# Attention heads on one core: 64-row value sums, a ring of scores, and a few tiles turned on TensorE

## The chip, the cores and the metric

The kernel runs on one core of a Trainium2 chip. The metric is device time in microseconds (us) of one execution; lower is better. The engines are TensorE (PE: matmuls, with its weight loads shown as PEld), VectorE (DVE), ScalarE (ACT), GpSimd (POOL) and SyncE (SP), which here issues most transfers (DMA).

## The reference, cut to what matters

The network has two layers over 3327 nodes with 256 features. Each layer is a graph step and a feed-forward step. Only the last step, the attention heads of layer 1, is touched by the change. With `s = 3327`, four heads (`n`) of width `d = 64`, and four query experts (`e`) per head it computes

```python
sx = einsum('bsh,ndh->bnsd', x, hl_w) + hl_b
pad = sx == 0
q = einsum('bnsd,neod->bneso', sx, wq)      # four queries per head
k = einsum('bnsd,nod->bnso', sx, wk)        # one key and one value per head
v = einsum('bnsd,nod->bnso', sx, wv)
causal = where(tril(ones((s, s))), 0, -inf)
# for every head and expert: softmax over the keys of (q . k scaled, causal), times v;
# a gate mixes the four experts, then layer norm, a small MLP, layer norm and a gate over heads
```

All of it is float32. The scores are a causal triangle: 26 query tiles of 128 rows, and query tile t needs the keys of tiles 0 to t. Over the four heads this makes 4 x (1 + 2 + ... + 26) = 1404 pairs of a query tile and a key tile, each with four experts. "Tile" below means one such pair.

## The kernel before, in words

The method is `heads`. Every engine takes its instructions strictly in the order in which the Python code issues them: the wrapper `InOrder` chains them, and it is why nearly every row of the profile carries the wrapper's line, L53. Rows are told apart by the names of their tiles.

A unit is one query tile t and one head h: 104 units, in the order of t and then h. Before, a unit's keys are cut into chunks of up to 512 (four key tiles); there are 392 chunks. For a chunk:

- `fill` makes the scores on PE: for each of four experts one matmul with 64 rows of contraction, 128 queries as weights and up to 512 keys moving. Experts in pairs use the two 64-row halves of the array side by side. On a unit's last chunk two small bfloat16 matmuls (`own`, `after`) add the causal mask. The four results (`pqk`) take four PSUM banks, which is the whole pool `ps`.
- `drain` copies each of the four to SBUF (`sc`) on DVE, which also takes the row's maximum (`TENSOR_SCALAR_CACHE_REDUCE`); after the last chunk a reduction makes the negated maximum `anmax`.
- `weigh` applies the exponential in place on ACT, one instruction per expert, with the row sum (`aden`).
- `turn` transposes 32 x 32 blocks of the chunk in place on DVE (`STREAM_TRANSPOSE`), so that keys lie on the partitions.
- `values` loads the chunk's values (`vr`) from DRAM (`vs`), four DMAs on SP.
- `attend` sums the values on PE into `po`: 32 keys of contraction, 64 value columns as weights, 128 columns (4 experts x 32 queries) moving. Eight such pieces of the array work side by side. Blocks above the diagonal are left out.

After a unit's last chunk `over` copies `po` to SBUF (`ot`, ACT) and masks it on POOL; in the following round `back` turns it with four matmuls (`ptO`) and ACT copies that out. `prepare` (projections of the next query tile: `xt2`, `sxt`, `pv`, `pk`, `pq`) and `tail` (gate, norms, MLP, output) are generators of which each round runs one step.

A float32 matmul runs as two passes, each with its own weight load, so the profile shows two records for one matmul; a transpose on PE (`pt<-ident`) shows one.

The main loop goes over the chunks; round k does, in this order: `drain` what is wanted ahead (filling first if needed), `attend(k)`, `turn(k + 1)`, `values(k + 2)`, half of `weigh(k + 2)`, `back`, `over`, one step of the tails and preparations, the other half of `weigh`, and the next `fill`.

Of the kernel before, what the change touches and what calls it, by code (L numbers as in the profile page):

```python
# [20 lines left out]
P = 128  # L21
# [72 lines left out]
class Net:  # L94
# [556 lines left out]
    def heads(self, xs, vs, out):  # L651
        tc, a = self.tc, self.a
        nc = InOrder(tc)
        Q = 32
        with ExitStack() as ctx:
            one = ctx.enter_context(tc.tile_pool(name="at", bufs=1))
            self.work = ctx.enter_context(tc.tile_pool(name="atw", bufs=2))
            scp = ctx.enter_context(tc.tile_pool(name="ats", bufs=9))
# [4 lines left out]
            ps = ctx.enter_context(tc.tile_pool(name="psm", bufs=4, space=PSUM))  # L663
# [44 lines left out]
            own = [one.tile([P, P], BF16, name=f"own{k}") for k in range(2)]  # L708
            after = [one.tile([P, P], BF16, name=f"after{k}") for k in range(2)]

            def where(t, op, base, sign=1):

                for k in range(2):
                    r = t[ds(64 * k, 64), :]
                    nc.gpsimd.affine_select(
                        out=r, in_=r, compare_op=op, fill=0.0, base=base,
                        pattern=[[sign, P]], channel_multiplier=-2 * sign,
                    )

            for k in range(2):  # L720
                nc.gpsimd.memset(own[k], 1.0)
                nc.gpsimd.memset(after[k], NEG)
            where(own[0], ALU.is_ge, 0)
            where(own[0], ALU.is_ge, 1, -1)
            where(after[0], ALU.is_ge, -2)
            where(own[1], ALU.is_equal, 0)
            where(after[1], ALU.is_equal, -1)

            kt = one.tile([P, 4, NP], F32, name="kt")
# [28 lines left out]
            def prepare(t, res):  # L758

                x = tl.tile([P, D], F32, tag="xres", name="xres", bufs=2)  # L760
# [15 lines left out]
                xt = self.work.tile([P, 2, P], F32, tag="xt", name="xt2")  # L776
# [8 lines left out]
                sxt = self.work.tile([P, 2, P], F32, tag="sxt", name="sxt")  # L785
# [7 lines left out]
                sxd = self.work.tile([P, 4, P], F32, tag="sxd", name="sxd", bufs=3)  # L793
# [21 lines left out]
                for s in range(2):  # L815
                    empty(kt[:, s::2, ts(t, P)], pp[s], D)
                for b in range(4):
                    nc.sync.dma_start(
                        out=vs[:, t // 4, :, 4 * (t % 4) + b, :].rearrange("h r d -> r h d"),
                        in_=v[ds(Q * b, Q), :, :],  # L820
                    )
# [14 lines left out]
                nc.vector.tensor_scalar(sxd, sxd, 0.0, None, ALU.not_equal)  # L836
# [3 lines left out]
                res.update(sx=sx, sxd=sxd, qt=qt)  # L840
# [9 lines left out]
            def fill(u, g):  # L850

                t, h = u["t"], u["h"]
                n = min(BLK, (t + 1) * P - g * BLK)
                last = g == t // 4
                pq = u["pq"] = []
                for i in range(2):
                    pq += [ps.tile([P, BLK], F32, tag="b", name="pqk") for _ in range(2)]
                    for k in range(2):
                        r = ds(64 * k, 64)
                        nc.tensor.matmul(  # L860
                            pq[2 * i + k][:, :n], u["qt"][r, h, i, :], kt[r, h, ds(g * BLK, n)],
                            start=True, stop=not last,
                        )
                    for m in range(2 if last else 0):
                        for k in range(2):
                            r = ds(64 * k, 64)
                            nc.tensor.matmul(
                                pq[2 * i + k][:, n - P : n], own[m][r, :], after[m][r, :],
                                start=False, stop=(m == 1),
                            )  # L870

            def drain(u, g):

                n = min(BLK, (u["t"] + 1) * P - g * BLK)
                if g == 0:
                    u["sc"] = {}
                    u["mx"] = sm.tile([P, 4, 8], F32, tag="mx", name="mx")
                sc = u["sc"][g] = scp.tile([P, 4, BLK], F32, tag="sc", name="sc")
                for e in range(4):
                    nc.vector.tensor_scalar(  # L880
                        sc[:, e, :n], u["pq"][e][:, :n], 1.0, None,
                        ALU.mult, ALU.max, accum_out=u["mx"][:, e, g : g + 1],
                    )
                    load["dve"] += 0.12 + 0.00104 * n
                if g == u["t"] // 4:
                    u["nmax"] = sm.tile([P, 4], F32, tag="nmax", name="anmax")
                    nc.vector.tensor_reduce(
                        u["nmax"], u["mx"][:, :, : g + 1], AX.X, ALU.max, negate=True
                    )
                    load["dve"] += 0.2  # L890

            def weigh(u, g, experts):

                n = min(BLK, (u["t"] + 1) * P - g * BLK)
                q = ready[u["t"]]
                if u["h"] == g == 0 and 0 in experts:
                    q["den"] = sm.tile([P, 16, 7], F32, tag="den", name="aden", bufs=3)
                for k in experts:
                    e = u["sc"][g][:, k, :n]
                    nc.scalar.activation(  # L900
                        e, e, AF.Exp, bias=u["nmax"][:, k : k + 1],
                        accum_out=q["den"][:, 4 * u["h"] + k, g : g + 1],
                    )
                    load["act"] += 0.26 + 0.00088 * n

            def values(u, g):

                n = 4 * min(4, u["t"] + 1 - 4 * g)
                v = u["v", g] = vrp.tile([P, 16, 64], F32, tag="vr", name="vr")
                for q in range(4):  # L910
                    nc.sync.dma_start(out=v[ds(Q * q, Q), :n, :], in_=vs[u["h"], g, :, :n, :])

            def turn(u, g):


                n = min(BLK, (u["t"] + 1) * P - g * BLK)
                w = u["sc"][g][:, :, :n]
                nc.vector.transpose(w, w)
                load["dve"] += 0.1 + 0.00417 * n


            po = ps_o.tile([P, 4, BLK], F32, tag="po", name="po")
            po = po[:, :, :P].rearrange("p q (e i) -> p q e i", e=4)

            def attend(u, g):


                t = u["t"]
                w, v = u["sc"][g], u["v", g]
                n = 4 * min(4, t + 1 - 4 * g)  # L930
                for b2 in range(0, n, 2):
                    for k in range(2):
                        for q in range(4):
                            r, b = ds(Q * q, Q), b2 + k

                            after = 4 * t + q - 16 * g
                            if b > after and t:
                                continue
                            nc.tensor.matmul(
                                po[ds(64 * k, 64), q, :, :], v[r, b, :], w[r, :, ts(b, Q)],  # L940
                                start=(g == b2 == 0), stop=(b + 2 > after if t else b2 == 2),
                            )

            def over(u):

                u["ot"] = tl.tile([P, 4, P], F32, tag="ot", name="ot", bufs=1)
                nc.scalar.copy(u["ot"].rearrange("p e (q i) -> p q e i", q=4), po)
                nc.gpsimd.tensor_tensor(
                    u["ot"], u["ot"],
                    u["sxd"][:, u["h"] : u["h"] + 1, :].to_broadcast([P, 4, P]), ALU.mult,  # L950
                )
                load["act"] += 0.6

            def back(u):
# [8 lines left out]
                for e in range(4):  # L963
                    nc.tensor.matmul(
                        pt[:, e, :], u["ot"][:, e, :], igw[:, h, e, :], start=True, stop=True
                    )
# [3 lines left out]
                if h == 3:  # L970
                    while len(tails) > 2:
                        run(tails)
                    tails.append(tail(u["t"], u["sx"], r["qkv"], r["glp"], r["den"]))
# [42 lines left out]
            def tail(t, sx, qkv, glp, den):  # L1016

                rd = sm.tile([P, 16], F32, tag="ard", name="ard")
                gl = sm.tile([P, 16], F32, tag="gl", name="gl")
                nc.vector.tensor_reduce(rd, den[:, :, : t // 4 + 1], AX.X, ALU.add)  # L1020
                nc.vector.reciprocal(rd, rd)
# [19 lines left out]
                fx = tl.tile([P, D], F32, tag="fx", name="fx", bufs=3)  # L1041
# [11 lines left out]
                h1 = tl.tile([P, 2, P], F32, tag="h1", name="h1")  # L1053
# [12 lines left out]
                fo = tl.tile([P, D], F32, tag="fo", name="fo", bufs=3)  # L1066
# [14 lines left out]
                x = tl.tile([P, D], F32, tag="xend", name="xend", bufs=2)  # L1081
# [28 lines left out]
            def fill_next():  # L1110
                nonlocal filled
                if filled < len(chunks):
                    u, g = chunks[filled]
                    if g == 0:
                        begin(u)
# [518 lines left out]
```

## Time and profile before

| | |
|---|---|
| time, median of 3 runs | 3280.33 us (3271.17 to 3280.51) |
| profiled execution | 3255.4 us, span 3253.7 us |
| mean granted PE clock | 0.945 |
| busy: PE, DVE, ACT, POOL | 2750.4, 2555.1, 1625.9, 876.6 us |
| heads, first to last `po` | 1123.9 to 3211.7 us of the span |
| query tiles 0 to 4 end at | 1305.2 us |
| then query tiles 5 to 25 end at | 3211.7 us |
| after that, the last tail alone | 42 us |

The profiled execution was 0.8% below the median of the three runs. Matmuls are pipelined and their recorded ends are modelled, so a PE that is shown busy is not a PE at its peak; starts of successive passes are the better measure. In the rows, `out<-in` names the tiles, and "x128" counts instructions.

### The profile page before, as it was taken

The page shows a single profiled execution, that of the slowest core. Times are in us where ns is not written, and L with a number is a line of the kernel's source. Part 1 is how long each engine was busy: PE and PEld are TensorE (multiplying, and loading weights), DVE is VectorE, ACT ScalarE, POOL GpSimd, SP SyncE. Part 2 cuts the span into 40 slices and gives each one's busy share as a digit, 9 for nine tenths or more (in the row PEclk, how much of TensorE's full clock was granted, in tenths as well). Part 3 has the DMA queues.
Part 4 walks back from the last instruction along what each step waited for, and adds up shares of the span by engine and source line. Part 5 has one row for each costly group of instructions (what it writes and reads, how often), then busy time and mean ns, then how long its engine had stood idle before and what let it go on. Part 6 is the DMA issues. An engine that isn't in the chain of part 4 may idle for free.

```text
span 3253.7 us, 126199 instructions
## 1 busy us (share of the span) xinstructions
PE 2750.4 (85%) x54213; PEld 2017.0 (62%) x54213; DVE 2555.1 (79%) x6382; ACT 1625.9 (50%) x4405; POOL 876.6 (27%) x1170
## 2 busy tenths in 40 slices
PE   5999959258898687999998998889998989999884
PEld 4888859236677565666665665656665655656553
DVE  4203555459999475888999999899999899999993
ACT  5410013045555354656666665556665566665662
POOL 3442532621112244433322222221121121111112
PEclk9999979689999787999999999999999999999997
DMA  9994523247675222333333333334333334433331
GB/s 339 322 293 134 181 80 134 89 149 256 232 278 187 78 77 65 97 94 96 109 105 98 105 108 104 94 102 110 107 109 104 97 103 113 113 109 103 109 102 52
DMA packets 247679, 434.19 MB, mean 133 GB/s; under 512 B 58288, under 2 KB 158128, under 8 KB 246992
## 3 DMA queue, kind: packets, MB, share of 16 engines
q1 hardware_dynamic: 227840, 393.36, 40.2%
q0 software_dynamic: 9456, 25.83, 2.3%
q8 instruction: 427, 7.00, 0.9%
q10 hardware_dynamic: 9824, 6.91, 0.7%
q14 instruction: 132, 1.08, 0.1%
HBM read 393.31 MB, written 25.82 MB: 129 GB/s over the span
## 4 chain that ended last, share of the span: by engine, by line
DVE 37%; PE 21%; ACT 2%; issue 2%; POOL 1%; DMA 0%; SPq 0%; POOLq 0%; DVEq 0%; ACTq 0%
DVE sc L53 32%; PE po L53 9%; PE pqk L53 8%; PE ptO L53 2%; ACT sc L53 2%; PE pq L53 1%; DVE l2mv L53 0%; PE pt L53 0%; DMA vr<-vs 0%; DVE l1mv L53 0%; PE ph L53 0%; DVE fo L53 0%; PE psxt L53 0%; DVE l2st L53 0%; DVE gl L53 0%
## 5 line engine op out<-in xcount | busy, mean ns | idle before, releaser
L53 ACT ACTIVATE sc<-sc,anmax 128x512 f32<-128x512 f32 (+3 forms) x1568 | 1041.3, 671 | 124.8 <-DVE anmax L53 124.8
L53 DVE TENSOR_SCALAR_CACHE_REDUCE sc<-pqk 128x512 f32<-128x512 f32 (+3 forms) x1568 | 898.7, 627 | 105.5 <-PE pqk L53 103.9
L53 PEld LDWEIGHTS po<-sc,vr 32*64 32x64 f32 x43728 | 675.6, 133 | 376.1 <-DVE sc L53 204.9
L53 PE MATMUL po<-sc,vr 32*64 32x128 f32 x43728 | 781.2, 279 | 128.0 <-DVE sc L53 61.7
L53 PE MATMUL pqk<-kt,qt 64*128 64x512 f32 (+3 forms) x3136 | 833.6, 585 | 55.4 <-DVE fo L53 17.2
L53 DVE STREAM_TRANSPOSE sc<-sc 128x2048 f32<-128x2048 f32 (+3 forms) x392 | 816.1, 2082 | 10.9 <-ACT sc L53 10.8
L53 PEld LDWEIGHTS pqk<-kt,qt 64*128 64x128 f32 x3136 | 321.2, 188 | 294.4 <-issue 120.5
L53 PE MATMUL acc<-wh,p 128*128 128x257 f32 x1352 | 307.0, 385 | 35.8 <-DVE p L53 35.6
L53 POOL TENSOR_TENSOR ot<-ot,sxd 128x512 f32<-128x512 f32 x104 | 132.7, 1276 | 689.8 <-ACT ot L53 659.3
L53 PEld LDWEIGHTS acc<-wh,p 128*128 128x128 f32 x1352 | 254.0, 191 | 91.0 <-DVE p L53 54.2
L53 PE MATMUL acc<-y,pan 128*128 128x256 f32 x1352 | 301.6, 385 | 5.8 <-DMA pan<-in_adjt_dram 4.1
L53 ACT ACTIVATION_READ_ACCUMULATOR sc<-sc,anmax 128x1 f32 x1568 | 303.6, 194 | 0.0
L53 PEld LDWEIGHTS acc<-y,pan 128*128 128x128 f32 x1352 | 259.9, 193 | 44.5 <-issue 8.1
L53 ACT ACTIVATE u<-u,d 128x512 f32<-128x512 f32 (+1 forms) x182 | 125.2, 688 | 156.4 <-DVE u L53 156.4
L53 ACT COPY qkv<-ptO 128x256 f32<-128x256 f32 x104 | 38.7, 372 | 276.9 <-PE ptO L53 276.9
L53 DVE SCALAR_TENSOR_TENSOR u<-bc,d 128x512 f32<-128x512 f32 (+1 forms) x182 | 135.0, 742 | 0.1
L53 DVE SCALAR_TENSOR_TENSOR p<-pan,u 128x512 f32<-128x512 f32 (+1 forms) x182 | 125.5, 689 | 9.9 <-PE acc L53 5.8
L53 DVE DVE_READ_ACCUMULATOR sc<-pqk 128x1 f32 x1568 | 129.1, 82 | 0.0
L53 PE MATMUL ptO<-igw,ot 128*128 128x68 f32 x832 | 117.3, 284 | 11.1 <-DVE sc L53 4.4
L53 PEld LDWEIGHTS ptO<-igw,ot 128*128 128x128 f32 x832 | 102.9, 194 | 30.9 <-issue 21.6
L53 ACT ACTIVATE junk<-ar 128x1664 bf16<-128x1664 f32 x52 | 82.7, 1591 | 52.8 <-DMA ar<-in_adj_dram 52.3
L53 POOL TENSOR_TENSOR qkv<-qkv,gss 128x1024 f32<-128x1024 f32 x26 | 50.0, 1924 | 210.0 <-DVE gss L53 210.0
(288 smaller groups left out, 2865.7 us busy)
## 6 DMA issues: line engine op xcount, KB each, us to landing
vr<-vs SPq DMA_DIRECT2D x1248, 128.0 KB, 2.8
ar<-in_adj_dram SPq DMA_DIRECT2D x104, 832.0 KB, 7.3
pan<-in_adjt_dram SPq DMA_DIRECT2D x156, 256.0 KB, 4.6
pan<-in_adjt_dram SPq DMA_DIRECT2D x26, 1024.0 KB, 10.8
pan<-in_adjt_dram SPq DMA_DIRECT2D x20, 832.0 KB, 4.6
vr<-vs SPq DMA_DIRECT2D x96, 96.0 KB, 2.3
took<-places SPq DMA_DIRECT2D x59, 128.0 KB, 2.0
made<-ye POOLq DMA_DIRECT2D x59, 128.0 KB, 2.0
```

What stands on the lines that cost most here:

```text
L53: made = make(*args, **kw)
```

## The change

All of it is in `heads`.

- Scores. The 128 partitions of a score tile now hold 64 queries beside two key halves: partition (q, a, i) is query 32q + i of the half s, with the keys 64a to 64a + 63 of every key tile. A unit's keys are cut into spans of up to 8 tiles. One piece of filling (a "bit") covers a span, two experts and one query half: eight matmuls of 64 rows by 32 weight columns, with 64 columns per key tile moving, into one of two PSUM buffers of two banks each (`ps_q`). The mask is two bfloat16 matmuls of full width per bit of the last span. There are 237 spans and 948 bits.
- The row maximum is now taken per key half (`half`), exchanged between the halves by a matmul with a permutation (`swap`, result `pn`) and combined on DVE (`top`). The row sums are likewise added over the halves by a matmul with `both`, in the tail.
- Scores lie in one ring of 41 tiles, `ring[P, 41, 8, 64]`; a span does not wrap.
- A round is now up to 4 tiles of a span: 442 rounds, of which 7, 43, 257 and 135 have 1, 2, 3 and 4 tiles. In the 392 rounds with 3 or 4 tiles the last tile is turned by four full 128 x 128 transposes on PE (`flip`, result `pf`) and copied back into the ring by ACT (`flipped`). The other 1012 tiles are turned on DVE as before.
- Value sums contract over 64 rows: per tile four matmuls of 64 x 64 with 256 columns moving, or, for a tile turned on PE, eight with 128 columns, into a second half of `po`. No block above the diagonal is left out any more.
- `over` copies up to 1024 columns on ACT, and POOL adds the two halves of `po` and masks them in four instructions instead of one.
- The pool `ps`, which the mask exchange, `pf`, `ptO`, preparations and tails share, has two banks instead of four. Values come with two DMAs per round, and four more where a tile is turned on PE.
- The rounds' filling and weighing are laid out ahead by `shared`, which spreads a unit's bits and exponentials over earlier rounds.

```diff
+        R = 41
+        WIDE = 8
...
-            scp = ctx.enter_context(tc.tile_pool(name="ats", bufs=9))
...
-            ps = ctx.enter_context(tc.tile_pool(name="psm", bufs=4, space=PSUM))
+            ps_q = ctx.enter_context(tc.tile_pool(name="psq", bufs=2, space=PSUM))
+            ps = ctx.enter_context(tc.tile_pool(name="psm", bufs=2, space=PSUM))
...
+            def fill(bit):
...
+                pq = bit["pq"] = ps_q.tile([P, 2, BLK], F32, tag="pq", name="pqk")
+                for q in range(2):
+                    for a in range(2):
                         for k in range(2):
                             r = ds(64 * k, 64)
                             nc.tensor.matmul(
+                                pq[ds(64 * q + Q * a, Q), k, : 64 * n],
+                                u["qt"][r, h, i, ds(64 * s + Q * q, Q)],
+                                kt[r, h, ds(t0, n), ds(64 * a, 64)],
+                                start=True, stop=True,
                             )
+                for k in range(2 if last else 0):
+                    r = ds(64 * k, 64)
+                    nc.tensor.matmul(
+                        pq[:, k, 64 * (n - 1) : 64 * n],
+                        own[s][r].rearrange("p q a i -> p (q a i)"), after[r, :],
+                        start=False, stop=True, skip_group_check=True,
+                    )
...
+            def other(u):
+                u["pn"] = ps.tile([P, 8], F32, tag="b", name="pn")
+                nc.tensor.matmul(
+                    u["pn"], swap.rearrange("p q a i -> p (q a i)"), u["half"], start=True, stop=True
+                )
+
+            def top(u):
+                u["nmax"] = sm.tile([P, 8], F32, tag="nmax", name="anmax")
+                nc.vector.tensor_tensor(u["nmax"], u["half"], u.pop("pn"), ALU.min)
...
+            def flip(rd):
+                w = scores(rd["span"], rd["t"] + rd["n"] - 1, 1)[:, 0, :, :]
+                pf = rd["pf"] = ps.tile([P, 4, P], F32, tag="b", name="pf")
+                for c in range(4):
+                    nc.tensor.transpose(
+                        pf[:, c, :], w[:, 2 * c : 2 * c + 2, :].rearrange("p r c -> p (r c)"),
+                        self.ident,
+                    )
+
+            def flipped(rd):
+                w = scores(rd["span"], rd["t"] + rd["n"] - 1, 1)[:, 0, :, :]
+                nc.scalar.copy(
+                    w.rearrange("p r c -> p (r c)"), rd.pop("pf").rearrange("p c x -> p (c x)")
+                )
...
+                for j in range(n - rd["flip"]):
+                    for b in range(2):
+                        for q in range(2):
+                            r = ds(64 * q, 64)
                             nc.tensor.matmul(
+                                po[ds(64 * b, 64), q, 0, :, :], v[r, j, b, :], w[r, j, :, ts(b, Q)],
+                                start=(t0 + j == 0), stop=last and j == n - 1 - rd["flip"],
+                                skip_group_check=True,
                             )
...
+            for k, rd in enumerate(rounds):
+                u = rd["span"]["u"]
+                tops()
+                n = len(fills[k])
+                drain_some(min(n, 2))
+                attend(rd)
+                then = rounds[k + 1] if k + 1 < len(rounds) else dict(flip=0)
+                if then["flip"]:
+                    flip(then)
+                if k + 1 < len(rounds):
+                    turn(then)
+                if n < 3:
+                    fill_ahead(new=False)
+                if k + 2 < len(rounds):
+                    values(rounds[k + 2])
+                h = len(weighs[k]) // 2
+                for w in weighs[k][:h]:
+                    weigh(*w)
+                if then["flip"]:
+                    flipped(then)
                 if ended:
                     back(ended)
...
+                fill_ahead()
+                compare()
```

## The prediction

> **What bounds the kernel now.** I read the busy times by stage first, since the change touches only the heads, then the costliest groups of the page, then one round of the timeline.
>
> ```profile
> 1120.00:1305.00 185.00, 150.97 (x2504) 112.70 (x2499) 121.04 (x420) 91.98 (x316) 76.40 (x83) 0.82 0.26 67
> 1305.00:3212.00 1907.00, 1721.43 (x47407) 1161.69 (x47406) 1773.76 (x4271) 1157.07 (x3475) 422.66 (x470) 0.99 0.38 104
> 3212.00:3254.00 42.00, 5.92 (x24) 4.33 (x24) 6.70 (x35) 2.39 (x8) 15.24 (x18) 0.54 0.01 4
> ```
>
> Columns: stage, length, busy PE, PEld, DVE, ACT, POOL, clock, DMA share. From 1305 us on (query tiles 5 to 25) DVE is busy 93% of the time, ACT 61%, and the granted clock is 0.99. DVE sets the pace; PE looks almost as full, but its ends are modelled, so I rebuild its need below.
>
> ```profile
> L53 ACT ACTIVATE sc<-sc,anmax 128x512 f32<-128x512 f32 (+3 forms) x1568 | 1041.3, 671 | 124.8 <-DVE anmax L53 124.8
> L53 DVE TENSOR_SCALAR_CACHE_REDUCE sc<-pqk 128x512 f32<-128x512 f32 (+3 forms) x1568 | 898.7, 627 | 105.5 <-PE pqk L53 103.9
> ...
> L53 PE MATMUL po<-sc,vr 32*64 32x128 f32 x43728 | 781.2, 279 | 128.0 <-DVE sc L53 61.7
> ...
> L53 DVE STREAM_TRANSPOSE sc<-sc 128x2048 f32<-128x2048 f32 (+3 forms) x392 | 816.1, 2082 | 10.9 <-ACT sc L53 10.8
> ```
>
> DVE's time is two things: draining scores (899) and turning (816). Its idle time is ended by PE's scores.
>
> ```profile
> 2707.70 2.31 DVE L53 STREAM_TRANSPOSE sc<-sc 128x2048 f32<-128x2048 f32 x1
> ...
> 2708.76 0.61 PE L53 MATMUL ptO<-igw,ot 128*128 128x68 f32 x4
> ...
> 2709.30 1.99 PE L53 MATMUL pqk<-kt,qt 64*128 64x512 f32 x8
> ...
> 2710.46 0.69 DVE L53 TENSOR_SCALAR_CACHE_REDUCE sc<-pqk 128x512 f32<-128x512 f32 x1 [0.45 <-PE pqk L53]
> ...
> 2711.22 2.10 PE L53 MATMUL po<-sc,vr 32*64 32x128 f32 x128
> ```
>
> A full chunk costs PE 1.92 for the scores (2709.30 to 2711.22) and 2.03 for the value sums (to the next operation at 2713.25). In the single records, passes of 512 columns start 0.43 apart, two at a time; 0.09 passes between the end of one kind of matmul and the first weight load of another shape, and 0.11 for that load: 0.11 + 4 x 0.43 + 0.09 = 1.92. So one column of one pass is 0.84 ns, and a change of shape costs 0.09 plus the load (0.03, 0.05, 0.11 for 32, 64, 128 columns). The value sums take (2.03 - 0.14) / 128 = 14.8 ns a pass.
>
> ```profile
> 1820.82 0.44 PE L53 MATMUL pt<-ident,sxt 128*128 128x128 f32 x2
> 1821.19 1.13 PE L53 MATMUL pqk<-kt,qt 64*128 64x512 f32 x4
> ```
>
> Two transposes hand over after 0.37 = 0.06 + 2 x 0.11 + 0.09: a transpose is 0.11.
>
> **DVE, part by part.** A drain shows 0.283, 0.415, 0.547 and 0.683 us for 128 to 512 columns, and starts every 0.61 at 512, so it costs 0.08 + 1.04 ns a column. Columns stay (512 per tile); instructions go from 1568 to 1896 (8 per span): +27. Turning: 0.702, 1.234, 1.769 us for one, two, three tiles; 7, 300 and 135 rounds turn so many: 614 against 816, so -202. `top` adds 104 x 0.17 = +18. Sum: **-157**.
>
> **PE, part by part**, before against after:
> - scores: 256 columns x 2 passes per tile, 0.43; 604 both times. After, this needs eight pieces of 64 x 32 at once. No row shows that shape; the nearest, eight of 32 x 64 in `po`, does run eight at once. I take that; the other end, four at once, costs +604.
> - value sums: 43,728 x 14.8 ns = 646; after, 256 columns x 2 passes again, 0.43 x 1404 = 608. Gain 38.
> - transposes: 392 x 4 x 0.11 = **+173**.
> - changes of shape, counted in the order of the instructions: 1049 x 0.174 = 182; after, 2288 x 0.142 = 326 (scores, mask, value sums and transposes all differ in shape). **+144**.
> - masks 23 to 12; `pn` and `pd` +26; `ptO` 92 and projections and tails 126 unchanged.
>
> Sum: 1673 before, **1967** after, +294. Before, PE had 2092 us for its 1673 (80%) and DVE set the end. After, PE needs 160 for query tiles 0 to 4 and 1807 for the rest, where DVE needs about 1774 - 150 = 1624. The bound moves from DVE to PE. The TensorE page of the Trainium skill ("TensorE: Matmul & The Clock Gate", Part 4) gives about 275 ns for a 128 x 128 transpose inside a kernel, against the 0.11 of successive starts here; by it the transposes would be 431 instead of 173 and the change 258 slower still. The same page (Part 1) says that starts never come closer than about 25 ns; the 14.8 ns here contradict it, and by it the 43,728 passes would need 1093 and the value sums gain 485 instead of 38.
>
> **What else moves.** ACT: 328 more exponentials at 0.289 us fixed (0.396 at 128 columns, 0.715 at 512) = +95; `flipped` is a copy of 512 PSUM columns, like `ot` at 0.573: 392 x 0.573 = +225; `over` copies 1024 columns, 0.97 by the rows for 256 and 512: +42. ACT goes to some 1500 of 1900: hidden behind PE on average, though it now sits in chains. POOL: four instructions of 0.73 instead of one of 1.28 per unit, +170, on an engine busy 423 of 1907: hidden unless `ptO` waits. SP: DMAs of values go from 1344 to 2452 at some 0.43 each to issue, 1.05 ms of 2; they are issued two rounds (7 us) ahead and landed in 2.8: hidden. If SP's queue fell behind, `attend` would wait; I give that nothing.
>
> **New waits on PE.** A typical round after (3 tiles, one of them turned on PE, two bits of 6 tiles): value sums 0.14 + 2 x 0.43 + 0.44 = 1.44, transposes 0.59, scores 0.12 + 2 x 0.645 = 1.41; 3.44 in all. DVE: four drains of 0.48 and a turn of 1.23, 3.15. Each is ready before PE needs it. Twice per unit it isn't:
> - `top` waits for `pn`, which stands behind the last scores on PE. The next drains and the next `turn` queue behind it on DVE: drains begin about 1.3 late, the turn ends near 4.0 instead of 2.7, and `attend` stalls 0.6 to 1.0. I take 0.8.
> - `over`'s copy now follows `flipped` on ACT and is 0.4 longer; it ends near 3.8 in the round while the next unit's `attend`, which overwrites `po`, wants to start at 3.44: 0.3 to 0.7. I take 0.5. Below nothing is excluded: both only add.
>
> 84 units of query tiles 5 to 25 x 1.3 = 109. In query tiles 0 to 4 PE had 185 us for 123 of work: 62 of waits, kept, plus 20 units x 1.0 = 82. After: 1967 + 109 + 82 = 2158 against 2092: **+66**, on the profiled execution 3255 + 66 = 3321. That execution ran 0.8% under the median of the runs, so against the median 3280 + 66 = **3346**. The change breaks even where PE's waits past 1305 us are 43 in all, 0.1 per round.
>
> **Rivals.**
> - PE binds but never waits longer (scores are double buffered now; before, one chunk took the whole pool): 1967 + 62 = 2029, -63, so **3217**. For it: DVE and ACT have slack on average. Against: before, the bound engine itself was only 93% busy. This is the case on the other side; it decides once the waits of 109 + 20 fall under the 43 + 20 above.
> - DVE stays the bound, because changes of shape hide behind queued work: -157 / 0.93 = -169, **3111**. Against: the 0.09 of handover appears at every change of shape in the trace.
> - The two banks of `ps`, shared by `pf`, `pn`, `ptO` and the rest, hold PE back: a bank is free only after ACT's copy, which queues behind exponentials of 0.6. At 0.25 a round, +110 more: **3456**.
> - The scores don't run eight at once: +604, **3950**. That the work on DVE doesn't fall as said is excluded by the counts.
>
> **How the numbers follow.** Forecast (PE bound, with its waits) 0.50; no new waits 0.22; DVE still bound 0.12; `ps` as well 0.12; four at once 0.04. The range, 3180 to 3480, takes in the first, second and fourth of these and leaves out 0.16 and small tails. The forecast's own range is 3282 to 3410 (the new waits of 129 at half and at one and a half times that). Runs shown lie 9 us apart, so 0.3% (10 us) is what can be told from no change; the band around 3280 gets 0.06 (0.03 each from the forecast and its first rival). Slower: 0.47 + 0.12 + 0.04 = 0.63, less 0.02 for the waits' lower ends: 0.61. Faster: 0.19 + 0.12 + 0.02 = 0.33.
>
> **What would show it.** Right: past the first fifth of the heads, DVE busy under 88%, PE's gaps small and ended by `turn` or ACT, transposes 392 x 4 with starts 0.11 apart, score passes of 6 tiles 0.32 apart in groups of eight. Wrong: DVE still above 92% (the bound did not move); score passes in two groups of four (+604); handovers between shapes under 0.09; waits of PE per round well over 0.3 with ACT or `pf` as releaser (the rival of `ps`), or none at all (the rival below zero).

## The result and the profile after

The changed kernel took 3512.61 us (median of 4 runs, 3507.89 to 3518.06) against 3275.75 for the kernel before on the same chip: a ratio of 1.0731, with an interval of 1.0691 to 1.0772. The forecast was 3346 in a range of 3180 to 3480. The direction and the new bound were right; the size was not, and the time lies above the range. The profiled execution spans 3507.2 us, 253 more than the one before; the medians are 237 apart, since the execution traced of the kernel before (3255) lay some 20 under its median.

The windows by stage come first (the columns are those of the windows before: stage, length, busy PE, PEld, DVE, ACT, POOL, clock, DMA share, GB/s).

```profile
1131.00:1394.00 263.00, 216.73 (x2720) 133.47 (x2712) 138.81 (x611) 120.89 (x452) 95.19 (x148) 0.68 0.13 31
1394.00:3463.00 2069.00, 1904.74 (x31742) 1061.32 (x31740) 1617.70 (x4904) 1467.14 (x4372) 553.78 (x823) 0.98 0.21 53
3463.00:3505.00 42.00, 6.25 (x28) 4.62 (x28) 6.96 (x36) 2.97 (x8) 16.72 (x21) 0.56 0.01 4
```

In query tiles 5 to 25 DVE is busy 1618 us, 156 less than before (forecast: 150), and only 78% of the stage. But the stage grew by 162, where the forecast had about 9 (1916 against 1907). Query tiles 0 to 4 grew by 78 (forecast: 57), and the heads start 12 later (forecast: nothing). Those 12 are not the change's: in the graph step ahead of the heads, which the change does not touch, the second run of the matmuls `acc` already starts at 754.0 us instead of 744.1. Such shifts between single traced executions come back below.

The costliest groups of the page (busy us, mean ns of one | idle time of the engine ahead of them, and what ended it):

```profile
L53 DVE TENSOR_SCALAR_CACHE_REDUCE ring<-pqk 128x384 f32<-128x384 f32 (+7 forms) x1896 | 936.4, 545 | 192.2 <-PE pqk L53 128.3
L53 PE MATMUL pqk<-kt,qt 64*32 64x384 f32 (+7 forms) x15168 | 813.0, 507 | 112.0 <-DVE ring L53 101.1
L53 DVE STREAM_TRANSPOSE ring<-ring 128x1024 f32<-128x1024 f32 (+2 forms) x442 | 615.9, 1394 | 105.9 <-ACT ring L53 105.8
...
L53 ACT COPY ring<-pf 128x512 f32<-128x512 f32 x392 | 226.5, 578 | 238.4 <-PE pf L53 237.6
...
L53 PE MATMUL pf<-ident,ring 128*128 128x128 f32 x1568 | 264.0, 290 | 2.0 <-ACT ring L53 1.8
```

The durations are the forecast ones: drains 936 (899 + 27 = 926 forecast), turning 616 (614), the copy `flipped` 0.578 each (0.573). PE stood idle only 2.0 us ahead of the transposes `pf`. One round in the timeline (start, length, operation) can be laid beside PE's prices:

```profile
2704.22 1.53 PE L53 MATMUL po<-ring,vr 64*64 64x256 f32 x24
...
2705.56 0.62 PE L53 MATMUL po<-ring,vf 64*64 64x128 f32 x16
...
2706.11 0.66 PE L53 MATMUL pf<-ident,ring 128*128 128x128 f32 x4
...
2706.70 0.77 PE L53 MATMUL pqk<-kt,qt 64*32 64x320 f32 x16
...
2707.40 0.20 PE L53 MATMUL pqk<-after,own 64*128 64x64 bf16 x2
```

Successive starts: four transposes hand over after 0.59 (2706.11 to 2706.70), a bit of five tiles after 0.70, near the 0.66 that 320 columns of two passes at 0.84 ns (0.54) and a change of shape (0.12) give; four pieces at once would need 1.08 for the columns alone. So the eight 64 x 32 pieces do run at once.

Where the time went instead shows in the waits (past 1394 us; us in total, times, longest):

```profile
DVE ring L53 <- PE pqk L53: 101.0, 115, 4.4
PE pqk L53 <- DVE ring L53: 85.8, 92, 9.0
...
DVE ring L53 <- POOL mx L53: 42.9, 15, 8.7
PEld ptO L53 <- POOL ot L53: 31.8, 32, 2.6
```

GpSimd, busy 29% of the span, appears twice: VectorE's drains wait for `mx`, up to 8.7 us at a time. The timeline at the longest of these:

```profile
1612.27 0.72 POOL L53 TENSOR_TENSOR fo<-fo,fng 128x256 f32<-128x256 f32 x1
...
1613.76 1.90 POOL L53 TENSOR_TENSOR qkv<-qkv,gss 128x1024 f32<-128x1024 f32 x1
...
1615.73 1.26 POOL L53 TENSOR_TENSOR qkv<-qkv 128x512 f32<-128x512 f32 x1
...
1618.67 0.12 POOL L53 MEMSET mx<- 128x32 f32 x1
1618.83 0.49 DVE L53 TENSOR_SCALAR_CACHE_REDUCE ring<-pqk 128x320 f32<-128x320 f32 x1 [8.72 <-POOL mx L53]
...
1619.89 2.39 PE L53 MATMUL pqk<-kt,qt 64*32 64x320 f32 x32 [8.97 <-DVE ring L53]
```

The change lets `begin` clear the table of maxima `mx` (and, once per query tile, `den`) by a memset on GpSimd, since the drains no longer write every entry. The memset itself takes 0.12 us. It stands behind the tail's operations in GpSimd's queue; the first drain of the unit waits for it, and the next scores wait for that drain's buffer: PE idle for 9 us. The kernel before had no such memset. The diff above is cut and doesn't hold the line; the prediction has no term for it.

### The profile page after: what moved, and what is told of

Same layout as the page of the kernel before. It is cut to its first block, busy times and chain, and to the rows that moved or that the text cites. A ratio compares the mean times of both kernels' runs of the same rounds, so it can differ in the third digit from the quotient of the medians.

```text
span 3507.2 us, 100357 instructions
## 1 busy us (share of the span) xinstructions
PE 3004.7 (86%) x38765; PEld 1940.4 (55%) x38765; DVE 2418.7 (69%) x7208; ACT 1965.4 (56%) x5437; POOL 1028.4 (29%) x1597
## 4 chain that ended last, share of the span: by engine, by line
PE 41%; DVE 12%; POOL 7%; ACT 5%; issue 3%; DMA 1%; SPq 0%; ACTq 0%; POOLq 0%; DVEq 0%
PE pqk L53 16%; PE po L53 12%; DVE ring L53 9%; PE pf L53 4%; ACT ring L53 3%; POOL ot L53 3%; PE ptO L53 3%; POOL fx L53 2%; POOL qkv L53 1%; POOL fo L53 1%; PE pq L53 1%; ACT o L53 1%; PE psxt L53 1%; PE ph L53 1%; PE pt L53 1%
## 5 line engine op out<-in xcount | busy, mean ns | idle before, releaser
L53 ACT ACTIVATE ring<-ring,anmax 128x384 f32<-128x384 f32 (+7 forms) x1896 | 1135.7, 606 | 121.5 <-DVE anmax L53 120.9
L53 DVE TENSOR_SCALAR_CACHE_REDUCE ring<-pqk 128x384 f32<-128x384 f32 (+7 forms) x1896 | 936.4, 545 | 192.2 <-PE pqk L53 128.3
L53 PE MATMUL pqk<-kt,qt 64*32 64x384 f32 (+7 forms) x15168 | 813.0, 507 | 112.0 <-DVE ring L53 101.1
L53 DVE STREAM_TRANSPOSE ring<-ring 128x1024 f32<-128x1024 f32 (+2 forms) x442 | 615.9, 1394 | 105.9 <-ACT ring L53 105.8
L53 PE MATMUL po<-ring,vr 64*64 64x256 f32 x8096 | 556.0, 397 | 28.7 <-ACT o L53 16.4
L53 PEld LDWEIGHTS po<-ring,vr 64*64 64x64 f32 x8096 | 273.0, 135 | 197.6 <-issue 33.2
L53 ACT ACTIVATION_READ_ACCUMULATOR ring<-ring,anmax 128x1 f32 x1896 | 366.5, 193 | 0.0
L53 ACT COPY ring<-pf 128x512 f32<-128x512 f32 x392 | 226.5, 578 | 238.4 <-PE pf L53 237.6
L53 PE MATMUL pf<-ident,ring 128*128 128x128 f32 x1568 | 264.0, 290 | 2.0 <-ACT ring L53 1.8
L53 PE MATMUL po<-ring,vf 64*64 64x128 f32 x6272 | 245.1, 271 | 0.7 <-ACT ring L53 0.5
```

Source lines behind the costliest of these rows:

```text
L53: made = make(*args, **kw)
```

## The experiments

Times are compared by the ratio to the kernel before in the same batch (its medians: 3277.49 in the first batch, 3267.52 in the second, 3278.39 in the third); 0.001 of ratio is 3.3 us.

| kernel | us | ratio | interval |
|---|---|---|---|
| changed kernel | 3512.61 | 1.0731 | 1.0691 to 1.0772 |
| no_flip | 3442.17 | 1.0508 | 1.0480 to 1.0537 |
| flip4 | 3462.10 | 1.0549 | 1.0521 to 1.0577 |
| no_exchange | 3476.50 | 1.0610 | 1.0587 to 1.0634 |
| mask_32 | 3468.88 | 1.0589 | 1.0563 to 1.0614 |
| mx_dve | 3427.96 | 1.0489 | 1.0462 to 1.0515 |
| mx_back | 3399.42 | 1.0405 | 1.0381 to 1.0430 |
| noex_mx | 3386.68 | 1.0370 | 1.0348 to 1.0393 |
| combo_b | 3315.87 | 1.0146 | 1.0128 to 1.0164 |
| early | 3416.59 | 1.0430 | 1.0400 to 1.0459 |
| all_flip | 3384.59 | 1.0329 | 1.0307 to 1.0352 |
| combo_c | 3329.18 | 1.0163 | 1.0142 to 1.0184 |
| combo_d | 3325.36 | 1.0153 | 1.0130 to 1.0176 |

**First batch: one part undone at a time.** Two theories stood against each other. A: each edit gives back the work that it takes from TensorE, and the waits stay. B: the waits around the edited part carry the loss, or another engine takes over as the bound.

*no_flip*: no tile is turned on TensorE.

```diff
-                        dict(span=span, t=span["t"] + t0, n=n, flip=int(n > 2))
+                        dict(span=span, t=span["t"] + t0, n=n, flip=int(n > 9))
```

> No tile is turned on TensorE: all 1404 are turned on VectorE. TensorE's own work falls by 226 us (1968 to 1742), VectorE's rises by about 202. Theory A (TensorE's work sets the pace and its waits of 375 us come on top): 3512 - 226 = about 3290. Theory B (the handovers between the engines set the pace; VectorE takes over as the longest engine): VectorE busy about 1820 us past the early query tiles, at the 93% of the kernel before 1957 instead of 2069, so about 3400. If the turning on TensorE is a gain in itself: above 3512.

Measured: 3442, 73 under the changed kernel by the ratios, where the work taken from TensorE was some 226. Both numbers were too low, and B's was nearer: past query tile 4 DVE is busy 1794 of 2006 us (89%). But the kernel before had about the same DVE work (1774) in 1907.

*flip4*: a tile is turned on TensorE only in rounds of four tiles (`n > 3`).

> Only rounds of four tiles turn their last tile on TensorE (135 instead of 392). TensorE's work falls by 150 us to 1818, VectorE's rises by about 137. Theory A: 3512 - 150 = 3362. Theory B: both engines near 1750 past the early tiles, neither far ahead, so 3380 to 3440. It also says whether the transposes have an optimum between all and none.

Measured: 3462, beyond both. Neither engine is full: DVE is busy 1716 and PE 1757 us in a stretch of 1986 (1394 to 3380 us). So engine totals do not explain the time; something makes all of them wait.

*no_exchange*: the halves don't exchange their maxima; each is scaled by its own.

```diff
-                nc.vector.tensor_tensor(u["nmax"], u["half"], u.pop("pn"), ALU.min)
+                u["nmax"] = u["half"]
...
-                for u in found:
-                    other(u)
+                return
```

> The row maximum is not exchanged between the key halves: each half is scaled by its own maximum (so the two halves' sums are no longer on one scale), and the matmul with the permutation and the VectorE step after it are left out. TensorE's work falls by 38 us to 1930. Theory A (only TensorE's work counts): 3512 - 38 = 3474. Theory B (VectorE stands still for that matmul's result, 102 us in the trace, and the drains, the turning and the exponentials queue behind it): 3512 - 38 - 70 to 100 = 3370 to 3405.

Measured: 3476, A's number. The exchange costs its work, and the wait for it is not where the loss lies. (The outputs are then not the reference's.) But in the waits past query tile 4, one line grew from 42.9:

```profile
DVE ring L53 <- POOL mx L53: 62.1, 20, 8.8
```

*mask_32*: the mask as eight 64 x 32 matmuls, of the scores' shape, instead of two of full width; 624 changes of shape fewer.

```diff
-                for k in range(2 if last else 0):
-                    r = ds(64 * k, 64)
-                    nc.tensor.matmul(
-                        pq[:, k, 64 * (n - 1) : 64 * n],
-                        own[s][r].rearrange("p q a i -> p (q a i)"), after[r, :],
...
+                for c in range(4 if last else 0):
+                    for k in range(2):
+                        r = ds(64 * k, 64)
+                        nc.tensor.matmul(
+                            pq[ds(Q * c, Q), k, 64 * (n - 1) : 64 * n],
+                            own[s][r, c // 2, c % 2, :], after[r, :],
...
```

> The causal mask is added by eight matmuls of 64 x 32 per bit, the shape of the scores, instead of two of 64 x 128: 1664 changes of shape instead of 2287, TensorE's work 1968 to 1891. If a change of shape costs what the prediction says and lies on the path: 3512 - 77 = 3435, at most 3400. If TensorE's waits absorb it: 3490 to 3512.

Measured: 3469, 47 under the changed kernel by the ratios. 29 of it lie ahead of query tile 5: the last `ptO` of query tile 4 ends at 1372.7 us instead of 1401.3. The clock granted over query tiles 0 to 4 rose with it, from 0.69 to 0.79.

**Second batch: GpSimd's queue.** New theory G: short work on GpSimd stands behind the tail's long work, and VectorE and TensorE wait for it. Rival H: handovers in general, where the next wait takes what one gives up.

*mx_dve*:

```diff
-                nc.gpsimd.memset(u["mx"], -3e38)
+                nc.vector.memset(u["mx"], -3e38)
```

> The memset of mx at the start of a unit is done by VectorE instead of GpSimd. In the changed kernel VectorE's first drain of a unit waits 59 us in all for this memset (20 waits, the longest 8.7), because it stands behind the tail's long operations in GpSimd's queue. Theory G (GpSimd's queue is on the path there, and the waits are lost time): 3450 to 3465, 45 to 60 under the changed kernel's 3512. Theory H (handovers between engines in general: what one wait gives up the next one takes): 3495 to 3515.

Measured: 3428, ratio 1.0489: 79 us gained by one word, more than the 59 of waits themselves. VectorE waits for `mx` no more, and PE's idle time ahead of the scores fell from 112 us to 66, as the page of mx_dve shows:

```profile
L53 PE MATMUL pqk<-kt,qt 64*32 64x384 f32 (+7 forms) x15168 | 802.5, 501 | 65.7 <-DVE ring L53 55.0
```

The two traced executions are also 79 apart (3507.2 and 3428.5). 10 of it lie ahead of the heads, whose first scores start at 1121.0 us instead of 1130.6, in work that the edit does not touch; 21 lie in query tiles 0 to 4 and 48 past them (to the last `ptO` of each stage), where the waits for `mx` were 43. H is out for this wait.

*mx_back*: in addition, the projection `ptO` of a finished unit later in the round.

```diff
-                if ended:
-                    back(ended)
+                was = ended
+                if was and u["t"] < 8:
+                    back(was)
...
+                if was and u["t"] >= 8:
+                    back(was)
                 fill_ahead()
                 compare()
```

> As mx_dve, and from query tile 8 on the projection ptO of a finished unit is issued at the end of the round instead of its middle, so that TensorE does not stand waiting for GpSimd's four operations on ot (waits of 57 us on matmuls and 36 on weight loads, partly the same ones, in the changed kernel). Theory G: 20 to 35 under mx_dve. Theory H: within 10 of mx_dve.

Measured: 28 less than mx_dve, as G expected, so the early place of `ptO`, behind GpSimd's four operations on `ot` (0.67 to 0.74 each), was on the path too. But PE's waits for `ot` ahead of `ptO` fell only from 26 us to 14; what else the later place gained was not taken apart.

*noex_mx*: no exchange, and `mx` on VectorE. The 83 in the expectation is the wait over the whole heads; past query tile 4 it was 62.

> The exchange of maxima between the halves is left out (swap, pn, top; each half is scaled by its own maxima, so the outputs are not the reference's), and the memset of mx is on VectorE. Without the exchange alone VectorE's waits for mx rose from 43 to 83 us past query tile 4. Theory G (they hid the gain): the two gains add and a little more, 3476 - 60 to 3476 - 85 = 3391 to 3416. Theory H: 3450 to 3476.

Measured: 3387, 39 under mx_dve, and just a little under G's range; the exchange alone had given 40. These two gains add.

*combo_b*: nothing turned on TensorE, the mask in 64 x 32 pieces, the waits on GpSimd taken away, `den`'s too, and `top` after two drains.

> Together: no tile turned on TensorE, the mask in 64x32 pieces, mx and den cleared on VectorE, ptO issued late, top after the first two drains of its round. If the single gains add (70 for the turning, 44 for the mask, 50 for the memset, 25 for ptO, 10 for top): 3512 - 199 = 3313. If VectorE, busy 1784 us past query tile 4 without the turning, binds as it did before the change (93% busy): 1918 there and 3330 in all. Theory H: 3370 to 3410.

Measured: 3316, still 1.0146 [1.0128, 1.0164] of the kernel before. The sum of single gains in the expectation (3313) came out by luck: it had 50 for the memset and 44 for the mask, which measured 79 and 47. By the measured ratios of no_flip, mask_32, mx_dve and mx_back the sum is 226 us, against 191 measured: the gains overlap by some 35. One traced execution of it, 19 us above the median (3335 against 3316), is read next. Its window past query tile 4, and the first line of the chain that ended last (the path of work followed back from the last instruction):

```profile
1362.00:3294.70 1932.70, 1667.26 (x29030) 856.02 (x29028) 1798.97 (x4986) 1232.86 (x3982) 422.74 (x552) 0.98 0.21 56
```

```profile
DVE 38%; PE 21%; ACT 3%; issue 2%; POOL 1%; DMA 1%; ACTq 0%; DVEq 0%; SPq 0%; POOLq 0%
```

With nothing turned on TensorE, DVE is busy 1799 of 1933 us: 93%, the share of the kernel before, and the chain reads as it did there:

```profile
DVE 37%; PE 21%; ACT 2%; issue 2%; POOL 1%; DMA 0%; SPq 0%; POOLq 0%; DVEq 0%; ACTq 0%
```

VectorE binds again, with 25 us more work than before. In the changed kernel this line of the page reads:

```profile
PE 41%; DVE 12%; POOL 7%; ACT 5%; issue 3%; DMA 1%; SPq 0%; ACTq 0%; POOLq 0%; DVEq 0%
```

GpSimd has 7% of the chain, some 250 us, against 1% before.

**Third batch: what is left.** *early*: mx_back, `igw` copied by VectorE, and the preparation two steps a round in query tiles 0 to 3.

```diff
-                        nc.gpsimd.tensor_copy(igw[r, h, e, :64], self.ident[r, r])
+                        nc.vector.tensor_copy(igw[r, h, e, :64], self.ident[r, r])
...
                     run(preps)
+                if u["t"] < 4:
+                    run(preps)
```

> As mx_back, and two edits ahead of query tile 5. The 32 copies of the identity into igw are made by VectorE (idle there) instead of GpSimd, where they take 5.9 us ahead of the power prs for which the first query tile waits. And in query tiles 0 to 3 the preparation of the next query tile advances two steps a round instead of one, since the first unit of each of these tiles takes 17 to 34 us where the other three take 6 to 9. Theory G (GpSimd's queue and the preparation are on the path there): -6 and some -25, 3368 against mx_back's 3399. Rival: the first units are long for work that the preparation does not cause, then -6 alone, 3393.

Measured: 3417, ratio 1.0430 [1.0400, 1.0459] against mx_back's 1.0405: no gain, a miss for both sides. In the traces the first scores started at 1133.5 us, in mx_back at 1120.3. This shift comes from ahead of the heads: the second run of the graph step's `acc` matmuls starts at 755.5 us here and at 742.8 there, and neither edit touches it. From the first scores to the last `ptO` the two take the same (2241 and 2239 us), so the edits gained nothing there either. Why the part ahead takes 10 to 20 us longer in some traced executions stays open.

*all_flip*: `mx`, `den` and `igw` on VectorE, `ptO` late, the mask in 64 x 32 pieces, `top` after two drains; tiles still turned on TensorE.

> The changed kernel as it stands (tiles still turned on TensorE), with mx and den cleared on VectorE, igw built on VectorE, the mask in 64x32 pieces, ptO late, top after two drains. mx_back measured 3399; the mask gave 44 when tried alone, top some 10, igw 6: 3339 if gains add, 3355 to 3375 if the mask's gain is partly the same time as the waits on GpSimd. Against combo_b (3316, nothing turned on TensorE) it tells whether turning a tile on TensorE pays once the waits on GpSimd are gone: if it is below 3310, it does.

Measured: 3385, by the ratio 25 under mx_back and so at the upper end of the overlapping forecast (3375 on mx_back's scale). Alone the mask had given 47. But part of the shortfall lies ahead of the heads, which start at 1139.7 us in this trace; from the first scores to the last `ptO` all_flip is 36 shorter than mx_back, where mask_32 was 49 shorter than the changed kernel. So the gains do overlap, but by some 13 us in the heads and not by all that the medians are short of. Turning tiles on TensorE costs 60 us against combo_b even with the waits for `mx` gone (1.0329 against 1.0146).

*combo_c* and *combo_d*: turned on TensorE only in rounds of four; and combo_d with the preparation two steps a round.

> As all_flip, but a tile is turned on TensorE only in rounds of four tiles (135 of 392 rounds). VectorE was the longest engine in combo_b, TensorE in mx_back. If the two only need balance, 3280 to 3300; if each transposed tile costs more in handovers than it spares VectorE, 3315 to 3335.

> As combo_c, and the preparation two steps a round in query tiles 0 to 3: 15 to 25 under combo_c if the preparation holds the first units up, the same if not.

Measured: 3329 and 3325, ratios 1.0163 and 1.0153, which can't be told from each other or from combo_b. In combo_d past query tile 4 both engines are at balance (DVE 1740, PE 1708 of 1914 us). That is 19 us shorter than combo_b's stage, but combo_b's traced execution was itself 19 above its median, and combo_d's 8 below; it is still above the 1907 before. Balance brings nothing that the medians show, and no version beats the kernel before.

## Why the prediction was right or wrong

**Right: the bound and the work.** DVE's work fell by 156 past query tile 4 (forecast: 150); over all heads by 138 (forecast: 157), since it rose by 18 in the longer query tiles 0 to 4. A count of the trace's instructions, each run of one shape at the prediction's prices, puts PE's work at about 149 us for query tiles 0 to 4 and 1812 after them, 1961; the forecast was 1967. That confirms the counts; the prices are confirmed by the round above: transposes, changes of shape, eight pieces at once, and by its row the copy `flipped`. The prediction's sum has one slip: 1404 tiles at 0.43 are 604 and not 608, which shifts it by 4. The Trainium skill's page "TensorE: Matmul & The Clock Gate" (Part 4) has about 275 ns for a transpose inside a kernel. As a duration the records agree (`pf` lasts 290 ns each), but successive ones start 0.11 us apart, and four with their change of shape took 0.59 us, so the price was the 0.11. The 14.8 ns a pass that the prediction sets against a floor of 25 are an average over eight pieces side by side; one piece takes a pass every 118 ns, so there is no contradiction.

**Wrong: the new waits on PE.** The stages less this work leave PE some 114 us of waits in query tiles 0 to 4 and 257 after them, about 370 in all (with whatever the prices miss, the slower clock of the first stage above all). The step "New waits on PE" had 62 + 20 and 109, 191 in all. It listed two waits per unit, of `top` and of `over`, and dismissed GpSimd with "+170, on an engine busy 423 of 1907: hidden unless `ptO` waits". That sentence is the one that failed, twice:
- it priced GpSimd by its load, not by its queue, and overlooked the memset of `mx` that the change adds to the start of every unit, for which VectorE waits: 79 us (mx_dve);
- its "unless" came true: `ptO` did wait for the four operations on `ot`; issuing it later gave 28 us (mx_back), of which PE's recorded waits for `ot` account for 12.

Together these are 107 of the 180 or so by which the waits were too low. Without them, at a ratio of 1.0405, the kernel is at 3399, inside the range given. In mx_back, past query tile 4:

```profile
1374.70:3360.00 1985.30, 1874.14 (x31642) 1053.37 (x31640) 1617.17 (x4973) 1465.14 (x4361) 546.67 (x740) 0.99 0.22 55
```

By the count PE's work is 1810 of these 1985 us (91%), so PE binds, as forecast; the 175 left for waits are still 66 above the 109 given. In the wait records, which overlap, `po` is held 31 us by `over`'s copy (forecast: 42) and 22 by turning, and `ptO` still 27 by `ot`. The rest was not taken apart, and its cause stays open.

**Too small: query tiles 0 to 4.** The forecast priced PE's 160 us there at the full clock. The chain of the changed kernel in this stage:

```profile
1163.23 3.10 PE pqk L53 x72
1166.33 0.52 PE pn L53 x2
1166.85 1.06 PE po L53 x8
1167.91 1.90 PE ptO L53 x8
1169.82 3.10 PE pqk L53 x72
```

A unit is PE alone, 6.59 us with nothing between; the clock granted from 1131 to 1180 us was 0.50, against 0.83 before (its 1119 to 1160). `ptO` takes 1.90 where it takes 1.04 at the full clock. In mask_32, with fewer changes of shape and a granted clock of 0.79 instead of 0.69, these five tiles end 29 us earlier. The stage grew by 78 where 57 were given; mx_dve, by the same mark on both, took 21 back.

**The rivals.** "DVE still bound" (3111) is excluded by DVE's 78%. "PE binds without new waits" (3217) is excluded by the waits: PE was idle 112 us ahead of the scores alone, where it had been 55. "`ps` as well" (3456) came nearest in time, but by another cause: PE was idle 2.0 us in all ahead of `pf`. "Four at once" is excluded by the 0.70 per bit. Of the signs of being wrong that the prediction named, PE's waits came to well over 0.3 a round (257 us past query tile 4, some 0.6 a round), but with VectorE and GpSimd as releasers in place of `pf`. The rival that was missing is the one that happened: a wait for an engine with 70% of its time free.

**Why the change loses at all.** Each half of the trade was measured by itself. Without turning on TensorE (combo_b) VectorE binds as before and has 25 us more to do past query tile 4, and query tiles 0 to 4 take 229 us instead of 192: slower by 1.5%. With it (all_flip), VectorE is some 150 us lighter than before, but PE has, by the prediction's prices, over 200 us more to do than before (294 in the changed kernel, 77 less with the mask in 64 x 32 pieces) and takes the bound: 60 us slower again. Balanced between them (combo_d) the kernel is as slow as combo_b: the stage past query tile 4 takes 1914 us, against 1904 before by the same mark, and query tiles 0 to 4 take 230.

## What to carry to other kernels

Price a step on a lightly used engine by what stands ahead of it in that engine's queue, not by the engine's load: list every new instruction there, memsets too, and ask who waits for it and what long work may be ahead. Moving 0.12 us of clearing per unit to another engine gave 2.4% here. And when work moves from the bound engine to the next one, both must be counted with their changes of shape and at the clock of the stage: the gain ends where the two meet.

## What the runs showed of the hardware

A TensorE that is never idle in the records may still be given half its clock: the windows of the changed kernel from 1160 to 1180 us, with columns as above.

```profile
1160.00:1170.00 10.00, 10.00 (x122) 6.38 (x123) 4.47 (x29) 5.48 (x28) 1.36 (x3) 0.50 0.09 23
1170.00:1180.00 10.00, 10.00 (x168) 5.52 (x152) 5.63 (x32) 6.43 (x30) 3.27 (x7) 0.50 0.08 20
```

The Trainium skill's page "TensorE: Matmul & The Clock Gate" (Part 1) has the clock rise after some 3.4 us of sustained work. Here it stayed at 0.50 from 1131 to 1200 us, 20 us of it with PE busy throughout. The matmuls there are short, with 8 to 256 columns and a change of shape every 0.2 to 2 us. In mask_32, where the mask has the scores' shape and so fewer changes come, the clock rises earlier, with PE less busy in the records:

```profile
1160.00:1170.00 10.00, 9.49 (x208) 7.15 (x204) 5.45 (x38) 6.59 (x33) 1.74 (x4) 0.67 0.12 32
1170.00:1180.00 10.00, 7.90 (x231) 5.89 (x216) 8.27 (x45) 9.18 (x44) 4.32 (x11) 1.00 0.06 16
```

The five kernels with the mask in this shape were granted 0.77 to 0.79 over query tiles 0 to 4, and the six that have the mask at full width and the exchange 0.66 to 0.73. So fewer changes of shape go with a higher clock here; what the clock answers to, these runs do not show.
